# All attention scores of a slice in one block of 96 matmuls over six PSUM banks

## The chip, the cores and the metric

The kernel runs on one core of one Trainium2 chip. The metric is the device time of one execution in microseconds (us), from runs of the whole program; a profile of one more execution shows where the time lies. The engines are called PE (TensorE), DVE (VectorE), ACT (ScalarE), POOL (GpSimd) and SP (SyncE). PE writes its results to PSUM, which has eight banks; DVE and ACT read them from there.

## What is computed

One layer of graph attention over 128 graphs of 128 nodes with 768 features, in 12 heads of 64. The adjacency matrix masks the scores and is added to them as a bias:

```python
# x: (128, 128, 768) f32, adj: (128, 128, 128) f32
h = maximum(layernorm(x), 0)
q, k, v = (split_heads(h @ W + b) for W, b in ((Wq, bq), (Wk, bk), (Wv, bv)))   # W: 768x768
scores = einsum('bhqd,bhkd->bhqk', q, k) / sqrt(64) + beta * adj
scores = where(adj > 0, scores, -9e15)
probs = softmax(scores, axis=-1)
out = x + merge_heads(einsum('bhqk,bhkd->bhqd', probs, v))
```

## The kernel before

The kernel works on 32 groups `G` of four graphs (512 rows). For each group it computes three slices in turn: `qk0` (queries and keys of heads 0 to 5), `v` (values) and `qk1` (queries and keys of heads 6 to 11). A slice is a 3x3 block matrix product by a scheme with 15 block products in place of 27: sums of blocks of activations (names S) and of weights (names T) are multiplied, and each product is added into one of four chains a, b, c, d, which lie in one PSUM bank each. Behind some products of a chain, ACT or DVE takes the chain's running sum into the tiles of the result.

```python
PRODUCTS = (                      # activations, weights, chain, ((block row, block column), sign)
    ("S9", "T9", "c", (((1, 1), -1),)),
    ("A10", "T12", "a", (((1, 0), -1),)),
    ("S10", "T10", "b", (((1, 0), 1),)),
    ("S2", "T2", "c", (((0, 1), -1),)),
    ("S8", "B12", "d", (((1, 1), -1), ((1, 2), 1))),
    # ... fifteen in all; the last of c, a and b are numbers 12, 13 and 14, of d number 8
)

psum = ctx.enter_context(tc.tile_pool(name="psum", bufs=4, space=bass.MemoryType.PSUM))

def product(G, sl, n):
    an, bn, chain, uses = PRODUCTS[n]
    first = all(p[2] != chain for p in PRODUCTS[:n])
    if first:
        banks[chain] = psum.tile([P, 2, H2], F32, tag="mm", name=f"p{chain}_{G}_{sl}")
    p = banks[chain]
    # ... 16 matmuls of 128 x 64 weights by 128 x 256, in halves q of 64 output partitions
    # ... then for each use: ACT (the first of a qk block) or DVE reads the bank
```

The pool has two tags of four banks: `mm` for the chains, `at` for all else (scores, weighted sums, the moments of the layernorm).

Two heads (`oc` is the pair's number) are handled by a pair of functions. `scores` computes query times key, in tiles of 64 x 64 (64 features of a head, 64 keys), for four graphs and two heads: 32 matmuls into two banks, which DVE adds the bias to and ACT takes the exponential of. `attend` multiplies by the values, with the row sum as a 65th column, and divides.

```python
def scores(G, oc):
    u, j = oc // 3, oc % 3
    t = xo[G, oc] = work.tile([P, GRP, P], F32, tag="xo", ...)        # x again, for the residual
    nc.sync.dma_start(t, x[...])
    ps = [psum.tile([P, GRP, N], F32, tag="at", name=f"sc_{G}_{oc}_{i}") for i in range(2)]
    for g in range(GRP):
        t = qk[G, f"qk{u}", g // 2, j]
        at = slice((g % 2) * N, (g % 2 + 1) * N)
        for i in range(2):
            r = slice(i * HD, (i + 1) * HD)
            for k in range(0, N, HD):
                nc.tensor.matmul(ps[i][k:k + HD, g, :], t[r, 1, at][:, k:k + HD], t[r, 0, at],
                                 start=True, stop=True)
    for i in range(2):
        e = es[G, oc, i] = work.tile([P, GRP, N], F32, tag="e", ...)   # four buffers
        nc.vector.scalar_tensor_tensor(e, ps[i], SCORE_CAP * ISCALE, biasT[G], op0=ALU.min, op1=ALU.add)
        nc.scalar.activation(e, e, AF.Exp, scale=1.0 / ISCALE)

def attend(G, oc):
    for r in range(2):
        pa = psum.tile([P, 4, VE], F32, tag="at", name=f"av_{G}_{oc}_{r}")
        # ... 16 matmuls of 128 x 64 weights (e) by 128 x 65 (values), then DVE: weigh()
    # ... POOL adds x, SP stores
```

These are placed between the products of a slice. Heads 0 to 5 (u = 0) of a group are handled in its slice `qk1`, heads 6 to 11 (u = 1) in slice `qk0` of the next group; slice `v` has no attention in it:

```python
def attention(G, u):
    todo = {}
    for i in range(3):
        todo.setdefault(1 + 4 * i, []).append(lambda oc=3 * u + i: scores(G, oc))            # after 1, 5, 9
        todo.setdefault(5 + 4 * i, []).insert(0, lambda oc=3 * u + i: attend(G, oc))         # after 5, 9, 13
    return todo

def slice_of(G, sl, todo, order=range(len(PRODUCTS))):
    for at, n in enumerate(order):
        product(G, sl, n)
        for f in todo.get(at, ()):
            f()
```

Beside this, the slices hold the preparation of the next group: `stats` (DVE, BATCH_NORM_STATS2) late in `qk0`, the moments (a few small matmuls, DVE, POOL) and `norm` (ACT) and the bias from the adjacency in `v`, the transposes of the normed x (DVE) and the sums of its blocks (DVE) in `qk1`. The framework orders the instructions of an engine by these places and by its own estimate of what is ready, so that work without a wait may stand a little earlier. The first group computes its `qk0` plainly (27 block products). The last group has no next slice for its heads 6 to 11 and handles them in half blocks (`scores_half`, 16 matmuls, line L405) within `qk1`.

Of the kernel before, what the change touches and what calls it, by code (L numbers as in the profile page):

```python
# [16 lines left out]
P = 128  # L17
HEADS = 12
GRP = 4
# [77 lines left out]
SLICES = ("qk0", "v", "qk1")  # L97

LAST = (0, 1, 2, 3, 5, 7, 6, 10, 11, 9, 4, 12, 8, 13, 14)

# [6 lines left out]
def direct(ctx, tc, x, adj, wq, bq, wk, bk, wv, bv, beta, out, bad):  # L107
# [27 lines left out]
    stat = ctx.enter_context(tc.tile_pool(name="stat", bufs=4))  # L135
    psum = ctx.enter_context(tc.tile_pool(name="psum", bufs=4, space=bass.MemoryType.PSUM))

# [86 lines left out]
    def moments_1(G, lo, hi):  # L224

        n = hi - lo
        pm[G, lo] = psum.tile([P, 2, n, 2], F32, tag="at", name=f"pm_{G}_{lo}")
        for q in range(0, P, HD):
            nc.tensor.matmul(pm[G, lo][q:q + HD, 0], mean8.rearrange("p a i -> p (a i)")[:, q:q + HD],
                             halves(G, lo, hi, 1), start=True, stop=True)  # L230
# [10 lines left out]
    def moments_2(G, lo, hi, mean, d):  # L241
# [5 lines left out]
        ve = stat.tile([P, n], F32, tag="ve", name=f"ve_{G}_{lo}", bufs=2)  # L247
        nc.vector.tensor_reduce(ve, pm[G, lo][:, 1], AX.X, ALU.add)
        nc.vector.tensor_scalar(ve, ve, -1.0, EPS, op0=ALU.mult, op1=ALU.add)
        r = stat.tile([P, n], F32, tag="rstd", name=f"rstd_{G}_{lo}", bufs=2)  # L250
# [53 lines left out]

    def product(G, sl, n):

        an, bn, chain, uses = PRODUCTS[n]
        first = all(p[2] != chain for p in PRODUCTS[:n])
        if first:
            banks[chain] = psum.tile([P, 2, H2], F32, tag="mm", name=f"p{chain}_{G}_{sl}")  # L310
        p = banks[chain]
        a, b = A[G, an], wt[sl, bn]
# [9 lines left out]
        for (r, j), sign in uses:  # L322
# [14 lines left out]
            elif key not in qk:  # L337
                t = qk[key] = work.tile([P, 2, H2], F32, tag="qk", name=f"{sl}_{G}_{r}_{j}", bufs=10)
                oc = j + 3 * int(sl[2])
# [3 lines left out]
            else:  # L343
                t = qk[key]
                added[G] = nc.vector.tensor_tensor(t, t, p, ALU.add if sign > 0 else ALU.subtract)  # L345

    es, xo = {}, {}

    def scores(G, oc):
        u, j = oc // 3, oc % 3  # L350
        t = xo[G, oc] = work.tile([P, GRP, P], F32, tag="xo", name=f"xo_{G}_{oc}", bufs=3)
        nc.sync.dma_start(t, x[G * GRP:(G + 1) * GRP, :, oc * P:(oc + 1) * P].rearrange("g n d -> n g d"))
        ps = [psum.tile([P, GRP, N], F32, tag="at", name=f"sc_{G}_{oc}_{i}") for i in range(2)]
        for g in range(GRP):
            t = qk[G, f"qk{u}", g // 2, j]
            at = slice((g % 2) * N, (g % 2 + 1) * N)
            for i in range(2):
                r = slice(i * HD, (i + 1) * HD)
                for k in range(0, N, HD):
                    nc.tensor.matmul(ps[i][k:k + HD, g, :], t[r, 1, at][:, k:k + HD], t[r, 0, at],  # L360
                                     start=True, stop=True)
        for i in range(2):
            e = es[G, oc, i] = work.tile([P, GRP, N], F32, tag="e", name=f"e_{G}_{oc}_{i}")
            nc.vector.scalar_tensor_tensor(e, ps[i], SCORE_CAP * ISCALE, biasT[G], op0=ALU.min, op1=ALU.add)  # L364
            nc.scalar.activation(e, e, AF.Exp, scale=1.0 / ISCALE)  # L365

# [11 lines left out]
    def attend(G, oc):  # L378
        o = work.tile([P, 2, 4, HD], F32, tag="o", name=f"o_{G}_{oc}", bufs=2)
        for r in range(2):  # L380
            pa = psum.tile([P, 4, VE], F32, tag="at", name=f"av_{G}_{oc}_{r}")
            for g in range(2):
                for i in range(2):
                    h = 2 * oc + i
                    for q in range(0, P, HD):
                        nc.tensor.matmul(pa[q:q + HD, 2 * g + i, :], es[G, oc, i][:, 2 * r + g, q:q + HD],  # L386
                                         vt[G, "v", r, h // 4][:, 4 * g + h % 4, :], start=True, stop=True)
            weigh(G, oc, r, pa, o[:, r])
        t = xo[G, oc]
        nc.gpsimd.tensor_add(t, t, o.rearrange("p a (b j) d -> p (a b) (j d)", j=2))  # L390
        nc.sync.dma_start(out[G * GRP:(G + 1) * GRP, :, oc * P:(oc + 1) * P].rearrange("g n d -> n g d"), t)

    def scores_half(G, oc, r):
# [4 lines left out]
        nc.sync.dma_start(t, x[g0:g0 + 2, :, oc * P:(oc + 1) * P].rearrange("g n d -> n g d"))  # L398
        ps = [psum.tile([P, 2, N], F32, tag="at", name=f"sc_{G}_{oc}_{r}_{i}") for i in range(2)]
        t = qk[G, f"qk{u}", r, j]  # L400
        for g in range(2):
            for i in range(2):
                h = slice(i * HD, (i + 1) * HD)
                for k in range(0, N, HD):
                    nc.tensor.matmul(ps[i][k:k + HD, g, :], t[h, 1, g * N + k:g * N + k + HD],  # L405
                                     t[h, 0, g * N:(g + 1) * N], start=True, stop=True)
        e = es[G, oc, r] = work.tile([P, 2, 2, N], F32, tag="e", name=f"e_{G}_{oc}_{r}")
        for i in range(2):
            nc.vector.scalar_tensor_tensor(e[:, i], ps[i], SCORE_CAP * ISCALE, biasT[G][:, 2 * r:2 * r + 2, :],
                                           op0=ALU.min, op1=ALU.add)  # L410
            nc.scalar.activation(e[:, i], e[:, i], AF.Exp, scale=1.0 / ISCALE)

    def attend_half(G, oc, r):
        o = work.tile([P, 4, HD], F32, tag="o", name=f"o_{G}_{oc}_{r}", bufs=2)
        pa = psum.tile([P, 4, VE], F32, tag="at", name=f"av_{G}_{oc}_{r}")
# [6 lines left out]
        weigh(G, oc, r, pa, o)  # L422
        t = xo[G, oc, r]
        nc.vector.tensor_add(t, t, o.rearrange("p (b j) d -> p b (j d)", j=2))
# [3 lines left out]
    def attention(G, u):  # L428

        todo = {}  # L430
        for i in range(3):
            todo.setdefault(1 + 4 * i, []).append(lambda oc=3 * u + i: scores(G, oc))
            todo.setdefault(5 + 4 * i, []).insert(0, lambda oc=3 * u + i: attend(G, oc))
        return todo

    def slice_of(G, sl, todo, order=range(len(PRODUCTS))):
        for at, n in enumerate(order):
            product(G, sl, n)
            for f in todo.get(at, ()):
                f()  # L440

    def plain_slice(G, sl, todo):

        n = 0
        for r in range(2):
            for j in range(3):
                p = psum.tile([P, 2, H2], F32, tag="mm", name=f"plain_{G}_{r}_{j}")
                for k in range(3):
# [6 lines left out]
                    if k == 2:  # L455
                        t = qk[G, sl, r, j] = work.tile([P, 2, H2], F32, tag="qk", name=f"{sl}_{G}_{r}_{j}", bufs=10)
                        oc = j + 3 * int(sl[2])
                        for i in range(2):
                            nc.scalar.activation(t[:, i, :], p[:, i, :], AF.Identity, bias=bqk[:, i, oc:oc + 1])
                    for f in todo.get(n, ()):  # L460
                        f()
# [35 lines left out]
    with tc.issue_after(squares[0].ins):  # L497
        warm = psum.tile([P, P], F32, tag="mm", name="warm")
        for n in range(10):
            nc.tensor.matmul(warm, ident, ident, start=True, stop=True)  # L500

# [5 lines left out]
    for G in range(NG):  # L507
        todo = attention(G - 1, 1) if G else {}

        def then(n, f):  # L510
            todo.setdefault(n, []).append(f)

        if G + 1 < NG:
# [15 lines left out]
        else:  # L529
# [3 lines left out]
            slice_of(G, "qk0", todo)  # L533
        todo = {}
        if G + 1 < NG:
            got = []
            at = 1 if G else 6
            for g in range(GRP):
# [12 lines left out]
        slice_of(G, "v", todo)  # L551
        todo = attention(G, 0)

        def transposes(n):
# [31 lines left out]
    nc.vector.tensor_scalar(over[:, 2:3], worst[:, 2:3], (BIAS_CAP * ISCALE) ** 2, None, op0=ALU.is_ge)  # L586
    pf = psum.tile([P, 4], F32, tag="mm", name="pf")
    nc.tensor.matmul(pf[0:1, 0:3], ones, over, start=True, stop=True)
# [133 lines left out]
```

## Time and profile before

| | |
|---|---|
| time, median of 3 runs | 2945.19 us (2944.01 to 2945.37) |
| span of the profiled execution | 2942.0 us |
| PE busy | 2920.4 us, 99% |
| DVE busy | 1993.9 us, 68% |
| ACT busy | 800.1 us, 27% |
| POOL busy | 374.9 us, 13% |
| score matmuls (L360) | 6048, and 96 in half blocks (L405) |
| evacuation of a score bank by DVE (L364) | 682 ns, 378 times |

In the lines of the profile, L320 is a block product, L360 a score matmul, L386 a weighted sum, L364 the DVE instruction that reads a score bank. "128*64" after a matmul is its tile: 128 rows of weights, 64 columns. Tiles are named by the program: pa_qk is chain a in a qk slice, sc a score bank, av a weighted sum, pm the moments. PEld is the loading of weights, which goes on beside the matmuls. Matmuls overlap each other, so the time that a stretch of them takes is read from start to start and not from the length of a line. An arrow points to what an instruction reads or to what it waited for.

### The profile page before, as it was taken

How to read it: one execution, taken by the hardware profiler on the slowest of the kernel's cores; microseconds unless marked ns; L12 is line 12 of the kernel's file. 1: busy time of each engine (PE TensorE's matmuls, PEld its weight loads, DVE VectorE, ACT ScalarE, POOL GpSimd, SP SyncE). 2: the span in 40 equal slices, each digit the busy share in tenths (PEclk: the TensorE clock that was granted, in tenths of full speed). 3: DMA queues.
4: the chain of work that ended last, by engine and by line, in shares of the span. 5: the costliest groups of instructions: out<-in, count | busy, mean ns of one | idle time of the engine just before them, and what ended most of it. 6: DMA issues, size and time to landing. Idle time of an engine off the chain costs nothing.

```text
span 2942.0 us, 81741 instructions
## 1 busy us (share of the span) xinstructions
PE 2920.4 (99%) x35526; PEld 2027.3 (69%) x35526; DVE 1993.9 (68%) x5155; ACT 800.1 (27%) x1703; POOL 374.9 (13%) x307
## 2 busy tenths in 40 slices
PE   8999999999999999999999999999999999999998
PEld 6666666666666666766666666666666676666666
DVE  7866667676676766776666767667676676666665
ACT  1322222323223222222222232222322223222221
POOL 1111111111111111101111111111111110111110
PEclk9999999999999999999999999999999999999999
DMA  5312122121221211221112212122121121211211
GB/s 160 73 52 54 49 63 67 54 55 45 58 70 52 60 47 52 70 61 53 52 47 67 66 52 59 43 60 70 52 59 46 53 69 56 59 47 45 66 38 41
DMA packets 358619, 172.20 MB, mean 59 GB/s; under 512 B 84464, under 2 KB 358128, under 8 KB 358256
## 3 DMA queue, kind: packets, MB, share of 16 engines
q1 hardware_dynamic: 355392, 166.14, 20.5%
q8 instruction: 280, 4.59, 0.6%
q10 hardware_dynamic: 2864, 0.79, 0.1%
q14 instruction: 83, 0.68, 0.1%
HBM read 116.53 MB, written 50.33 MB: 57 GB/s over the span
## 4 chain that ended last, share of the span: by engine, by line
PE 95%; issue 2%; DVE 1%; DMA 1%; ACT 0%; POOL 0%; SPq 0%; POOLq 0%; DVEq 0%
PE pc_qk L320 18%; PE pa_qk L320 15%; PE pb_qk L320 15%; PE pc_v L320 9%; PE pa_v L320 7%; PE pb_v L320 7%; PE pd_qk L320 7%; PE sc L360 6%; PE av L386 6%; PE pd_v L320 4%; PE plain L452 1%; DMA x<-in_x_dram 0%; DVE A L269 0%; ACT x L262 0%; POOL rstd L251 0%
## 5 line engine op out<-in xcount | busy, mean ns | idle before, releaser
L390 POOL TENSOR_TENSOR xo<-xo,o 128x512 f32<-128x512 f32 x189 | 257.0, 1360 | 2266.9 <-DVE seen L376 2208.8
L365 ACT ACTIVATE e<-e 128x512 f32<-128x512 f32 x378 | 232.1, 631 | 713.2 <-DVE e L364 712.4
L262 ACT ACTIVATE x<-x,shift,rstd 128x192 f32<-128x192 f32 x512 | 228.0, 533 | 545.6 <-POOL shift L253 545.6
L320 PE MATMUL pb_qk<-S,qk_T 128*64 128x256 f32 x3024 | 361.7, 381 | 0.0
L341 ACT ACTIVATE qk<-pc_qk,bqk 128x256 f32<-128x256 f32 x378 | 157.6, 467 | 634.9 <-PE pc_qk L320 634.9
L364 DVE SCALAR_TENSOR_TENSOR e<-sc,biasT 128x512 f32<-128x512 f32 x378 | 242.2, 682 | 57.2 <-PE sc L360 57.1
L320 PEld LDWEIGHTS pb_qk<-S,qk_T 128*64 128x64 f32 x3024 | 206.0, 137 | 102.0 <-issue 8.9
L345 DVE TENSOR_TENSOR qk<-qk,pb_qk 128x512 f32<-128x512 f32 x252 | 172.0, 683 | 120.0 <-PE pb_qk L320 119.4
L320 PE MATMUL pc_qk<-S,qk_B 128*64 128x256 f32 x2016 | 243.7, 384 | 3.5 <-ACT qk L341 3.5
L320 PE MATMUL pa_qk<-S,qk_T 128*64 128x256 f32 x2016 | 242.2, 382 | 0.0
L320 PE MATMUL pc_qk<-S,qk_T 128*64 128x256 f32 x2016 | 239.4, 379 | 0.0
L386 PEld LDWEIGHTS av<-v,e 128*64 128x64 f32 x6048 | 208.9, 138 | 27.6 <-issue 0.4
L269 DVE STREAM_TRANSPOSE A<-x 128x256 f32<-128x256 f32 x384 | 218.4, 614 | 7.5 <-ACT x L262 7.4
L360 PE MATMUL sc<-qk 64*64 64x128 f32 x6048 | 208.7, 275 | 0.0
L386 PE MATMUL av<-v,e 128*64 128x65 f32 x6048 | 208.5, 221 | 0.0
L320 PEld LDWEIGHTS pc_qk<-S,qk_T 128*64 128x64 f32 x2016 | 145.0, 137 | 72.8
L320 PEld LDWEIGHTS pc_qk<-S,qk_B 128*64 128x64 f32 x2016 | 139.5, 137 | 79.1 <-issue 11.6
L320 PEld LDWEIGHTS pa_qk<-S,qk_T 128*64 128x64 f32 x2016 | 138.9, 137 | 74.7 <-issue 11.0
L360 PEld LDWEIGHTS sc<-qk 64*64 64x64 f32 x6048 | 163.0, 132 | 32.9 <-issue 24.2
L320 PE MATMUL pb_v<-v_T,S 128*64 128x256 f32 x1536 | 183.4, 380 | 0.0
L219 DVE BATCH_NORM_STATS2 st<-x 128x6 f32<-128x192 f32 x512 | 153.1, 346 | 43.2 <-DMA x<-in_x_dram 38.7
L345 DVE TENSOR_TENSOR qk<-qk,pd_qk 128x512 f32<-128x512 f32 x126 | 86.2, 684 | 129.1 <-PE pd_qk L320 129.1
(117 smaller groups left out, 4221.4 us busy)
## 6 DMA issues: line engine op xcount, KB each, us to landing
x<-in_x_dram SPq DMA_DIRECT2D x504, 96.0 KB, 2.3
xo<-in_x_dram SPq DMA_DIRECT2D x189, 256.0 KB, 2.7
out_dram<-xo SPq DMA_DIRECT2D x189, 256.0 KB, 2.2
adj<-in_adj_dram SPq DMA_DIRECT2D x128, 64.0 KB, 2.4
qk_T<-in_L_gnn_Wq_dram SPq DMA_DIRECT2D x10, 128.0 KB, 3.3
qk_T<-in_L_gnn_Wk_dram SPq DMA_DIRECT2D x10, 128.0 KB, 3.2
v_T<-in_L_gnn_Wv_dram SPq DMA_DIRECT2D x5, 256.0 KB, 5.8
qk_B<-in_L_gnn_Wq_dram SPq DMA_DIRECT2D x8, 128.0 KB, 3.3
```

The lines of the kernel that those rows point to most:

```text
L219: nc.vector.bn_stats(st[G][:, g * NB + b, :], xg[G, g][:, b, :])
L262: nc.scalar.activation(t, t, AF.Relu, bias=shift[G, n], scale=rstd[G, n])
L269: last = nc.vector.transpose(t[:, :, g * N:(g + 1) * N].rearrange("p c (b i) -> p c b i", i=SQ), src)
L320: nc.tensor.matmul(p[q:q + HD, i, :], lhs[:, q:q + HD], rhs, start=(first and i == 0 and c == 0), stop=(c == 1), skip_group_check=True)
L341: nc.scalar.activation(t[:, i, :], p[:, i, :], AF.Identity, bias=bqk[:, i, oc:oc + 1], scale=float(sign))
L345: added[G] = nc.vector.tensor_tensor(t, t, p, ALU.add if sign > 0 else ALU.subtract)
L360: nc.tensor.matmul(ps[i][k:k + HD, g, :], t[r, 1, at][:, k:k + HD], t[r, 0, at], start=True, stop=True)
L364: nc.vector.scalar_tensor_tensor(e, ps[i], SCORE_CAP * ISCALE, biasT[G], op0=ALU.min, op1=ALU.add)
L365: nc.scalar.activation(e, e, AF.Exp, scale=1.0 / ISCALE)
L386: nc.tensor.matmul(pa[q:q + HD, 2 * g + i, :], es[G, oc, i][:, 2 * r + g, q:q + HD], vt[G, "v", r, h // 4][:, 4 * g + h % 4, :], start=Tru ...
L390: nc.gpsimd.tensor_add(t, t, o.rearrange("p a (b j) d -> p (a b) (j d)", j=2))
L452: nc.tensor.matmul(p[:, i, :], b[:, c, i * P:(i + 1) * P], a[:, c, :], start=(k == 0 and i == 0 and c == 0), stop=(c == 1), skip_group_che ...
```

## The change

The three score functions of a slice (three pairs of heads, 32 matmuls each) become one, placed after the second product of the next slice: heads 0 to 5 in slice `v` of the same group (in the first group, in `qk1`), heads 6 to 11 in `qk0` of the next group, as before. It takes six PSUM banks at once and issues 96 score matmuls in a row. It is for having fewer changes between the products' tiles and those of the scores. So that six banks are to be had, the two tags of four banks are given up: the kernel hands out all eight from one queue, and gives each back when its last reader is issued. `attend` goes to places 5, 8 and 11 of the slice. The e buffers become six, the qk buffers eight (from ten), and in slice `v` the moments move from places 1 and 3 to 3 and 6.

```diff
+SC_AT = 1
+AV_AT = (5, 8, 11)
...
-    psum = ctx.enter_context(tc.tile_pool(name="psum", bufs=4, space=bass.MemoryType.PSUM))
+    psum = ctx.enter_context(tc.tile_pool(name="psum", bufs=1, space=bass.MemoryType.PSUM))
+    free = deque(psum.tile([P, W], F32, name=f"bank{i}") for i in range(8))
+    take, give = free.popleft, free.append
... product():
+        mine = [i for i in order if PRODUCTS[i][2] == chain]
+        first = n == mine[0]
         if first:
-            banks[chain] = psum.tile([P, 2, H2], F32, tag="mm", name=f"p{chain}_{G}_{sl}")
+            banks[chain] = take()
...
+        if n == mine[-1]:
+            give(banks.pop(chain))
...
-    def scores(G, oc):
+    def scores(G, u):
+        order = (3 * u, 3 * u + 2, 3 * u + 1)
+        ps = {(oc, i): take() for oc in order for i in range(2)}
+        for oc in order:
+            for g in range(GRP):
+                # ... the same 32 matmuls
             for i in range(2):
-            e = es[G, oc, i] = work.tile([P, GRP, N], F32, tag="e", name=f"e_{G}_{oc}_{i}")
+                e = es[G, oc, i] = work.tile([P, GRP, N], F32, tag="e", name=f"e_{G}_{oc}_{i}", bufs=6)
+                nc.vector.scalar_tensor_tensor(e, ps[oc, i]..., SCORE_CAP * ISCALE, biasT[G], ...)
+                give(ps[oc, i])
+                nc.scalar.activation(e, e, AF.Exp, scale=1.0 / ISCALE)
... attention():
-        for i in range(3):
-            todo.setdefault(1 + 4 * i, []).append(lambda oc=3 * u + i: scores(G, oc))
-            todo.setdefault(5 + 4 * i, []).insert(0, lambda oc=3 * u + i: attend(G, oc))
+        for i, oc in enumerate((3 * u, 3 * u + 2, 3 * u + 1)):
+            todo.setdefault(AV_AT[i] - 3, []).append(lambda oc=oc: load_xo(G, oc))
+            todo.setdefault(AV_AT[i], []).append(lambda oc=oc: attend(G, oc))
... the loop over groups, slice qk0:
+        if G:
+            todo.setdefault(SC_AT, []).insert(0, lambda: scores(G - 1, 1))
... slice v:
-        todo = {}
+        todo = {SC_AT: [lambda: scores(G, 0)]} if G else {}
-            at = 1 if G else 6
+            at = 3 if G else 6
-            then(at + 2, lambda: moments_2(G + 1, 0, GRP * NB, *got[:2]))
+            then(at + (3 if G else 2), lambda: moments_2(G + 1, 0, GRP * NB, *got[:2]))
... slice qk1:
+        if not G:
+            todo.setdefault(SC_AT, []).insert(0, lambda: scores(0, 0))
... slice qk1 of the last group:
-            (0, scores, 0), (3, attend, 0), (3, scores, 1), (6, attend, 1), (6, scores, 2), (9, attend, 2),
+            (0, load_xo, 0), (0, load_xo, 1), (0, load_xo, 2), (0, attend, 0), (2, attend, 2), (4, attend, 1),
```

The rest of the diff makes the other users of PSUM (moments, weighted sums, half blocks, the plain slice) take and give their banks in the same way.

More of the change, by code (lines that the diff above doesn't have):

```diff
@@ L1 @@
 import math
+from collections import deque
 from contextlib import ExitStack
@@ L226, in moments_1 @@
         n = hi - lo
-        pm[G, lo] = psum.tile([P, 2, n, 2], F32, tag="at", name=f"pm_{G}_{lo}")
+        bank = pm[G, lo, "bank"] = take()
+        pm[G, lo] = bank[:, 0:4 * n].rearrange("p (s b h) -> p s b h", s=2, h=2)
         for q in range(0, P, HD):
@@ L248, in moments_2 @@
         nc.vector.tensor_reduce(ve, pm[G, lo][:, 1], AX.X, ALU.add)
+        give(pm[G, lo, "bank"])
         nc.vector.tensor_scalar(ve, ve, -1.0, EPS, op0=ALU.mult, op1=ALU.add)
@@ L303, in direct, with product @@
     banks, added = {}, {}
-    def product(G, sl, n):
+    def product(G, sl, n, order):
         an, bn, chain, uses = PRODUCTS[n]
-        first = all(p[2] != chain for p in PRODUCTS[:n])
+        mine = [i for i in order if PRODUCTS[i][2] == chain]
+        first = n == mine[0]
         if first:
-            banks[chain] = psum.tile([P, 2, H2], F32, tag="mm", name=f"p{chain}_{G}_{sl}")
-        p = banks[chain]
+            banks[chain] = take()
+        p = banks[chain].rearrange("p (i w) -> p i w", i=2)
         a, b = A[G, an], wt[sl, bn]
@@ L337, in product @@
             elif key not in qk:
-                t = qk[key] = work.tile([P, 2, H2], F32, tag="qk", name=f"{sl}_{G}_{r}_{j}", bufs=10)
+                t = qk[key] = work.tile([P, 2, H2], F32, tag="qk", name=f"{sl}_{G}_{r}_{j}", bufs=8)
                 oc = j + 3 * int(sl[2])
@@ L345, in product, with load_xo @@
                 added[G] = nc.vector.tensor_tensor(t, t, p, ALU.add if sign > 0 else ALU.subtract)
+        if n == mine[-1]:
+            give(banks.pop(chain))
     es, xo = {}, {}
-    def scores(G, oc):
-        u, j = oc // 3, oc % 3
+    def load_xo(G, oc):
         t = xo[G, oc] = work.tile([P, GRP, P], F32, tag="xo", name=f"xo_{G}_{oc}", bufs=3)
         nc.sync.dma_start(t, x[G * GRP:(G + 1) * GRP, :, oc * P:(oc + 1) * P].rearrange("g n d -> n g d"))
[L353 to L356, printed above, removed]
-            for i in range(2):
[L358 to L362, printed above, removed]
-            e = es[G, oc, i] = work.tile([P, GRP, N], F32, tag="e", name=f"e_{G}_{oc}_{i}")
-            nc.vector.scalar_tensor_tensor(e, ps[i], SCORE_CAP * ISCALE, biasT[G], op0=ALU.min, op1=ALU.add)
-            nc.scalar.activation(e, e, AF.Exp, scale=1.0 / ISCALE)
+    def scores(G, u):
[3 more added lines that the diff above has]
+            for g in range(GRP):
+                t = qk[G, f"qk{u}", g // 2, oc % 3]
+                at = slice((g % 2) * N, (g % 2 + 1) * N)
+                for i in range(2):
+                    r = slice(i * HD, (i + 1) * HD)
+                    for k in range(0, N, HD):
+                        nc.tensor.matmul(ps[oc, i][k:k + HD, g * N:(g + 1) * N], t[r, 1, at][:, k:k + HD], t[r, 0, at],
+                                         start=True, stop=True)
+            for i in range(2):
+                e = es[G, oc, i] = work.tile([P, GRP, N], F32, tag="e", name=f"e_{G}_{oc}_{i}", bufs=6)
+                nc.vector.scalar_tensor_tensor(e, ps[oc, i].rearrange("p (g n) -> p g n", g=GRP), SCORE_CAP * ISCALE,
+                                               biasT[G], op0=ALU.min, op1=ALU.add)
+                give(ps[oc, i])
+                nc.scalar.activation(e, e, AF.Exp, scale=1.0 / ISCALE)
     def weigh(G, oc, r, pa, o):
@@ L380, in attend @@
         for r in range(2):
-            pa = psum.tile([P, 4, VE], F32, tag="at", name=f"av_{G}_{oc}_{r}")
+            bank = take()
+            pa = bank[:, 0:4 * VE].rearrange("p (b e) -> p b e", e=VE)
             for g in range(2):
@@ L388, in attend @@
             weigh(G, oc, r, pa, o[:, r])
+            give(bank)
         t = xo[G, oc]
@@ L398, in scores_half @@
         nc.sync.dma_start(t, x[g0:g0 + 2, :, oc * P:(oc + 1) * P].rearrange("g n d -> n g d"))
-        ps = [psum.tile([P, 2, N], F32, tag="at", name=f"sc_{G}_{oc}_{r}_{i}") for i in range(2)]
+        ps = [take() for i in range(2)]
         t = qk[G, f"qk{u}", r, j]
@@ L404, in scores_half @@
                 for k in range(0, N, HD):
-                    nc.tensor.matmul(ps[i][k:k + HD, g, :], t[h, 1, g * N + k:g * N + k + HD],
+                    nc.tensor.matmul(ps[i][k:k + HD, g * N:(g + 1) * N], t[h, 1, g * N + k:g * N + k + HD],
                                      t[h, 0, g * N:(g + 1) * N], start=True, stop=True)
-        e = es[G, oc, r] = work.tile([P, 2, 2, N], F32, tag="e", name=f"e_{G}_{oc}_{r}")
+        e = es[G, oc, r] = work.tile([P, 2, 2, N], F32, tag="e", name=f"e_{G}_{oc}_{r}", bufs=6)
         for i in range(2):
-            nc.vector.scalar_tensor_tensor(e[:, i], ps[i], SCORE_CAP * ISCALE, biasT[G][:, 2 * r:2 * r + 2, :],
+            nc.vector.scalar_tensor_tensor(e[:, i], ps[i][:, 0:2 * N].rearrange("p (g n) -> p g n", g=2), SCORE_CAP * ISCALE, biasT[G][:, 2 * r:2 * r + 2, :],
                                            op0=ALU.min, op1=ALU.add)
+            give(ps[i])
             nc.scalar.activation(e[:, i], e[:, i], AF.Exp, scale=1.0 / ISCALE)
@@ L414, in attend_half @@
         o = work.tile([P, 4, HD], F32, tag="o", name=f"o_{G}_{oc}_{r}", bufs=2)
-        pa = psum.tile([P, 4, VE], F32, tag="at", name=f"av_{G}_{oc}_{r}")
+        bank = take()
+        pa = bank[:, 0:4 * VE].rearrange("p (b e) -> p b e", e=VE)
         for g in range(2):
@@ L422, in attend_half @@
         weigh(G, oc, r, pa, o)
+        give(bank)
         t = xo[G, oc, r]
@@ L437, in slice_of @@
         for at, n in enumerate(order):
-            product(G, sl, n)
+            product(G, sl, n, order)
             for f in todo.get(at, ()):
@@ L446, in plain_slice @@
             for j in range(3):
-                p = psum.tile([P, 2, H2], F32, tag="mm", name=f"plain_{G}_{r}_{j}")
+                bank = take()
+                p = bank.rearrange("p (i w) -> p i w", i=2)
                 for k in range(3):
@@ L455, in plain_slice @@
                     if k == 2:
-                        t = qk[G, sl, r, j] = work.tile([P, 2, H2], F32, tag="qk", name=f"{sl}_{G}_{r}_{j}", bufs=10)
+                        t = qk[G, sl, r, j] = work.tile([P, 2, H2], F32, tag="qk", name=f"{sl}_{G}_{r}_{j}", bufs=8)
                         oc = j + 3 * int(sl[2])
@@ L459, in plain_slice @@
                             nc.scalar.activation(t[:, i, :], p[:, i, :], AF.Identity, bias=bqk[:, i, oc:oc + 1])
+                        give(bank)
                     for f in todo.get(n, ()):
@@ L497, in direct @@
     with tc.issue_after(squares[0].ins):
-        warm = psum.tile([P, P], F32, tag="mm", name="warm")
+        warm = take()
         for n in range(10):
-            nc.tensor.matmul(warm, ident, ident, start=True, stop=True)
+            nc.tensor.matmul(warm[:, 0:P], ident, ident, start=True, stop=True)
+        give(warm)
     def behind_adds(f, *args):
@@ L586, in direct @@
     nc.vector.tensor_scalar(over[:, 2:3], worst[:, 2:3], (BIAS_CAP * ISCALE) ** 2, None, op0=ALU.is_ge)
-    pf = psum.tile([P, 4], F32, tag="mm", name="pf")
+    pf = take()
     nc.tensor.matmul(pf[0:1, 0:3], ones, over, start=True, stop=True)
```

## The prediction

> **What bounds the kernel now.** I read the page first, then the waits of TensorE, the timeline of TensorE over one steady slice and over the end, a table of busy time by stage, and the timeline of VectorE. The page:
>
> ```profile
> span 2942.0 us, 81741 instructions
> PE 2920.4 (99%) x35526; PEld 2027.3 (69%) x35526; DVE 1993.9 (68%) x5155; ACT 800.1 (27%) x1703; POOL 374.9 (13%) x307
> ...
> PEclk9999999999999999999999999999999999999999
> ...
> PE 95%; issue 2%; DVE 1%; DMA 1%; ACT 0%; POOL 0%; SPq 0%; POOLq 0%; DVEq 0%
> PE pc_qk L320 18%; PE pa_qk L320 15%; PE pb_qk L320 15%; PE pc_v L320 9%; PE pa_v L320 7%; PE pb_v L320 7%; PE pd_qk L320 7%; PE sc L360 6%; PE av L386 6%; PE pd_v L320 4%; PE plain L452 1%; DMA x<-in_x_dram 0%; DVE A L269 0%; ACT x L262 0%; POOL rstd L251 0%
> ```
>
> TensorE is on 95% of the chain that ended last, at full clock throughout. Its list of waits begins so (columns: total us, times, longest us):
>
> ```profile
> PE pm L229 <- DVE st L219: 7.1, 2, 5.7
> PE pc_qk L320 <- ACT qk L341: 3.5, 1, 3.5
> ```
>
> These are its two longest waits, and both lie in the first 100 us. In the steady part TensorE waits for nobody: time can be won only by giving TensorE less to do or by losing less between its instructions. A busy matmul row does not show such losses, because matmuls overlap; the start times do. The timeline of TensorE at the border of slices qk1 and qk0 (columns: start us, length us, then the instructions merged):
>
> ```profile
> 1018.70 1.10 PE L386 MATMUL av<-v,e 128*64 128x65 f32 x32
> 1019.63 1.90 PE L320 MATMUL pb_qk<-S,qk_T 128*64 128x256 f32 x16
> 1021.36 1.90 PE L320 MATMUL pc_qk<-S,qk_T 128*64 128x256 f32 x16
> 1023.09 1.90 PE L320 MATMUL pa_qk<-A,qk_T 128*64 128x256 f32 x16
> 1024.92 1.10 PE L360 MATMUL sc<-qk 64*64 64x128 f32 x32
> 1025.95 1.95 PE L320 MATMUL pb_qk<-S,qk_T 128*64 128x256 f32 x16
> 1027.73 1.90 PE L320 MATMUL pc_qk<-S,qk_T 128*64 128x256 f32 x16
> ```
>
> From start to start a product of 16 matmuls takes 1.727 us among other products (1021.36 to 1023.09), but 1.827 us when a score block follows (1023.09 to 1024.92: 0.100 us more) and 1.778 us when one came before (1025.95 to 1027.73: 0.051 us more). The weighted sums (av) have the same 128*64 tile as the products and cost no such extra: 1018.70 to 1019.63 is 0.932 us, and the product behind it is again 1.73. Only the scores have the form 64*64.
>
> What a score block costs inside I take from two sizes. One oc has 32 matmuls and takes 1.034 us (1024.92 to 1025.95). The last group has half blocks of 16, here by their starts:
>
> ```profile
> 2917.03 0.67 PE L405 MATMUL sc<-qk 64*64 64x128 f32 x16
> 2917.62 1.95 PE L320 MATMUL pd_qk<-S,qk_B 128*64 128x256 f32 x16
> ```
>
> That is 0.598 us for 16 (the starts unrounded). Sixteen more matmuls cost 1.034 - 0.598 = 0.436 us, or 27.25 ns each, and the part that does not grow is 0.598 - 0.436 = 0.162 us. The single starts in the trace agree: within a block, four matmuls go by every 109 ns, without a break where the block passes to another qk tile.
>
> **What the Trainium skill says.** "TensorEngine Tiling (Array Packing)", Tiling Modes, Key Properties: changing the tiling mode, and not just the tile, drains TensorE. The trace agrees, and gives the price the page lacks: 0.100 + 0.162 + 0.051 = 0.313 us for going into 64*64 and out again. "TensorE: Matmul & The Clock Gate", Part 3, says matmuls on separate tiles run side by side, starting about 4 ns apart; here the four of a group start 6 to 7 ns apart and the next four 109 ns after the first. So the score work itself is already packed, and only the drains are to be won. "PSUM — Partial Sum Buffer", Specifications, gives eight banks of 512 fp32 values a partition: a block of six score banks leaves two for product chains, which is the change's danger.
>
> **What the change removes.** Scores of 189 oc blocks of 32 (6048 / 32) become 63 blocks of 96: 32 for slice qk0 and 31 for qk1 (the last group's qk1 keeps its half blocks). Each takes 0.162 + 96 x 0.02725 = 2.778 us inside, in place of 3 x 1.034 = 3.102, and two of three exits and entries fall away. Per block of 96: 2 x 0.313 = 0.626 us less. 63 x 0.626 = 39.4 us, all on the path, since TensorE is the path. The number of matmuls, weight loads, evacuations and transfers stays.
>
> **What it adds: waits for banks.** Products 0 and 1 of a slice take two banks, the scores six, so product 2 (chain b) must take the bank the first scores leave. Let T be the start of the block. The first two banks are full after 32 matmuls, T + 1.10 us. VectorE empties one in 0.68 us: free at about T + 1.85 if VectorE comes at once. TensorE needs it at T + 2.78. The slack is 0.9 us. Later takers have more: the second score bank is wanted two products later (+3.5 us) and VectorE frees a bank every 0.6 to 0.7 us. At the front the scores need banks of chains c, a and b of the slice before; they are taken last in the block, and chain b's last product was over two products (3.5 us) before the block starts, so VectorE has some 5 us for one 0.68 us instruction.
>
> Does VectorE come at once? By start times over all 31 first score blocks of qk0 slices, the first evacuation starts 1.14 us after the block's start in the median and 1.57 us in nine of ten; later only at the launch. The busy time by stage (a qk0, a v and a qk1 slice; columns: us, then busy time and count of PE, PEld, DVE, ACT, POOL, then clock and DMA):
>
> ```profile
> 1021.36:1053.62 32.26, 32.26 (x435) 22.66 (x432) 22.80 (x71) 9.23 (x19) 4.32 (x5) 1.00 0.24 65
> 1053.62:1079.76 26.14, 26.14 (x252) 17.28 (x250) 11.88 (x22) 7.12 (x16) 4.39 (x3) 1.00 0.07 21
> 1079.76:1112.02 32.26, 32.26 (x436) 22.68 (x434) 28.00 (x71) 8.61 (x18) 3.01 (x2) 1.00 0.29 83
> ```
>
> **What it moves.** The scores of heads 0 to 5 go from slice qk1, where VectorE is fullest (28.0 of 32.26 us), to v, where it is emptiest (11.9 of 26.14). Six evacuations are 6 x 0.68 = 4.1 us. After: qk1 some 23.9 of 32.26 - 3 x (1.034 + 0.151) = 28.7 us; v some 16.0 of 26.14 + 2.93 = 29.07 us; qk0 22.8 of 31.63. No stage comes near to full on VectorE. In v, VectorE now waits for each product:
>
> ```profile
> 1076.52 0.69 DVE L336 TENSOR_TENSOR v<-v,pc_v 128x512 f32<-128x512 f32 x1 [1.04 <-PE pc_v L320]
> 1078.24 0.69 DVE L336 TENSOR_TENSOR v<-v,pa_v 128x512 f32<-128x512 f32 x1 [1.04 <-PE pa_v L320]
> ```
>
> so it will meet the block there at once. ACT does the exponentials early (six of 0.63 us = 3.8) and then the norm, which now starts two to three products later because the moments moved from 1 to 3 and from 3 to 6. By the sum (moments after seven products and the block, about 15.1 us into the slice; 4 us for variance and power; 16 x 0.53 us = 8.5 of norm) it ends near 27.7 us of 29.1. That is close, but it feeds transposes of qk1 whose results TensorE needs only in the next qk0. Three xo loads and stores a slice move too, far from any limit (2.7 us to landing).
>
> **The rivals.**
> 1. A bank wait takes the drains' place. VectorE's queue is in order, and other work may be put ahead of the score evacuations: four BATCH_NORM_STATS2 (1.1 us) or four transposes (2.2 us). If that happened in every qk0 slice, product 2 would wait up to 1.3 us: 31 x 1.3 = 40 us, and the time would be unchanged near 2945. Against it: the median of 1.14 us above. For it: at 1026.0 four such stats did stand ahead of the scores, and the first came 2.14 us after the block's start (free then at T + 2.85: a wait of about 0.1 us).
> 2. The 0.162 us inside a block belongs to each oc (new banks), not to the change of form. Then only 0.151 us is saved 126 times: 19 us, 2926. Against it: the matmuls of a block pass between two banks all the time and cross qk tiles at the same 109 ns.
> 3. The launch gets worse. Between 80 and 125 us VectorE is the bound (it meets the first scores 5.3 us after their start), so the saving is worth nothing there, and six score banks held longer could add 2 to 5 us.
> 4. More than the drains is won. TensorE's waits in all are some 16 us, most of it before 100 us or at the very end; there is nothing else to win, so 2% (59 us) is out of reach.
>
> **The number.** 2945.2 - 39.4 = 2905.8; the launch and a few tenths of a wait in some slices I put at +2: **2908 us**, a ratio of 0.987. The low end, 2900, is the drains in full and a few us of luck at the launch; the high end, 2926, is rival 2, or rival 1 at half strength. Chances: faster by over 2% 0.03, within 2% 0.93, slower by over 2% 0.04 (rival 1 in both v and qk0 with something I don't see).
>
> **What would show it.** Right: 63 score blocks of 96, with 2.78 us to the next start, 1.83 us for the product ahead and 1.78 for the one behind; a period of 90.66 - 2 x 0.626 = 89.41 us for a group of four graphs; no wait of TensorE for VectorE's score evacuation behind a block. Wrong: a gap ahead of product 2 (pb) ended by VectorE; score blocks cut up by products or moments; block time that grows by more than 2.78; a new wait for chain banks at the slice's front.

## The result, and the profile after

The changed kernel takes 2915.24 us (median of 4 runs, 2913.27 to 2918.47) against 2944.6 us before: a ratio of 0.9901, with a 95% interval of 0.9884 to 0.9919. That is 29 us less; the prediction had 2908 and a range of 2900 to 2926. The head of the page of the changed kernel:

```profile
span 2913.8 us, 81848 instructions
PE 2881.5 (99%) x35526; PEld 2017.0 (69%) x35526; DVE 1993.8 (68%) x5155; ACT 796.6 (27%) x1703; POOL 376.0 (13%) x307
```

The counts of instructions and the busy time of DVE are the same. PE has 39 us less, though not one matmul fewer: its row counted the pauses at the change of form as busy. The waits of PE (total us, times, longest us); all users of PSUM are called `bank` now, L331 is a product and L381 the evacuation of a score bank:

```profile
PE bank L331 <- DVE e L381: 11.9, 11, 3.6
PE bank L238 <- DVE st L227: 7.7, 2, 5.8
PE bank L331 <- DVE qk L356: 2.5, 7, 0.9
```

The first line is new: products that wait until DVE has emptied a score bank. The timeline of PE (start us, length us) at a block of 96 (L377) in slice qk0, and then at one in slice v:

```profile
1016.41 1.90 PE L331 MATMUL bank<-A,qk_T 128*64 128x256 f32 x16
1018.24 2.85 PE L377 MATMUL bank<-qk 64*64 64x128 f32 x96
1021.42 3.67 PE L331 MATMUL bank<-S,qk_T 128*64 128x256 f32 x32 [0.33 <-DVE e L381]
...
1048.45 1.90 PE L331 MATMUL bank<-v_T,A 128*64 128x256 f32 x16
1050.27 2.85 PE L377 MATMUL bank<-qk 64*64 64x128 f32 x96
1053.05 3.67 PE L331 MATMUL bank<-v_T,S 128*64 128x256 f32 x32
```

In v the block takes 2.78 us to the next start and the product ahead of it 1.83 us. In qk0 here it is 3.18 us: 0.40 us more, of which the trace puts 0.33 down to the wait for a bank. Over all 63 blocks the medians are 1.827 us for the product ahead, 2.781 us for the block and 1.778 us for the product behind. The busy time by stage, a qk0, a v and a qk1 slice (us; then PE, PEld, DVE, ACT, POOL with counts, clock, DMA):

```profile
1014.69:1046.72 32.03, 31.70 (x434) 22.41 (x432) 22.18 (x64) 9.07 (x19) 5.07 (x5) 1.00 0.30 77
1046.72:1075.78 29.06, 29.06 (x346) 19.97 (x344) 15.52 (x28) 10.75 (x22) 3.13 (x2) 1.00 0.04 11
1075.78:1104.49 28.71, 28.71 (x339) 20.14 (x337) 24.50 (x70) 5.04 (x12) 4.29 (x3) 1.00 0.30 83
```

v and qk1 last what was reckoned (29.07 and 28.7), and VectorE's load has moved from qk1 to v. qk0 is 0.4 us over its 31.63.

To compare the kernels I cut each trace at the starts of products. "Launch" is from the first v product of group 0 to the v slice of group 1. "Steady" is from there to the v slice of group 31 (30 groups, 60 score slices). What is ahead of the launch part differs by up to 3 us from trace to trace (47.7 to 50.8 us), also between kernels that are the same there, and nothing is read from it.

| kernel | us, median | launch | steady | waits in steady qk0, qk1 |
|---|---|---|---|---|
| before | 2944.6 | 96.7 | 2720.2 | 0.0, 1.0 |
| after | 2915.2 | 101.4 | 2690.7 | 5.9, 2.6 |
| banks_only | 2944.0 | 96.1 | 2721.1 | 0.0, 1.9 |
| three_blocks | 2945.8 | 97.6 | 2721.6 | 0.0, 2.1 |
| two_blocks | 2922.4 | 97.4 | 2700.7 | 0.0, 0.0 |
| block_at_0 | 2909.0 | 99.4 | 2683.8 | 0.0, 1.8 |
| stats_behind | 2905.8 | 98.2 | 2682.0 | 0.0, 0.0 |
| behind_and_0 | 2905.6 | 98.5 | 2682.0 | 0.0, 0.0 |
| a12_early | 2909.9 | 102.6 | 2684.1 | 2.1, 0.0 |
| launch_three | 2912.5 | 97.7 | 2689.8 | 6.2, 1.5 |
| behind_launch | 2905.0 | 97.6 | 2682.0 | 0.0, 0.0 |
| form_128 | 3046.4 | 98.6 | 2822.8 | 0.0, 2.3 |

The waits are sums of what the slices take above the median of their kind. In the kernel after, the steady part is 29.5 us shorter, and the launch part 4.7 us longer.

### The profile page after: what moved, and what is told of

Read it like the earlier page. It is cut to its first block, busy times and chain, and to the rows that moved or that the text cites. A ratio compares the mean times of both kernels' runs of the same rounds, so it can differ in the third digit from the quotient of the medians.

```text
span 2913.8 us, 81848 instructions
## 1 busy us (share of the span) xinstructions
PE 2881.5 (99%) x35526; PEld 2017.0 (69%) x35526; DVE 1993.8 (68%) x5155; ACT 796.6 (27%) x1703; POOL 376.0 (13%) x307
## 4 chain that ended last, share of the span: by engine, by line
PE 81%; issue 8%; DVE 5%; DMA 2%; POOL 2%; SPq 1%; ACT 0%; ACTq 0%; POOLq 0%; DVEq 0%
PE bank L331 70%; PE bank L406 5%; PE bank L377 5%; DMA x<-in_x_dram 2%; DVE S L285 1%; PE bank L477 1%; POOL xo L411 1%; POOL rstd L261 1%; DVE qk L356 1%; DVE st L227 1%; DVE A L279 1%; DVE o L392 0%; SPq L152 0%; DVE e L381 0%; ACT x L272 0%
## 5 line engine op out<-in xcount | busy, mean ns | idle before, releaser
L331 PE MATMUL bank<-S,qk_T 128*64 128x256 f32 x7056 | 825.5, 380 | 13.3 <-DVE e L381 11.9
L331 PEld LDWEIGHTS bank<-S,qk_T 128*64 128x64 f32 x7056 | 503.9, 137 | 273.4 <-DVE e L381 16.4
L356 DVE TENSOR_TENSOR qk<-qk,bank 128x512 f32<-128x512 f32 x630 | 430.4, 683 | 347.0 <-PE bank L331 346.7
L352 ACT ACTIVATE qk<-bank,bqk 128x256 f32<-128x256 f32 x756 | 313.4, 471 | 1010.4 <-PE bank L331 870.1
L331 PE MATMUL bank<-S,qk_B 128*64 128x256 f32 x4032 | 478.1, 379 | 0.9 <-DVE qk L356 0.9
L331 PE MATMUL bank<-A,qk_T 128*64 128x256 f32 x4032 | 478.5, 379 | 0.3 <-DVE qk L356 0.3
L331 PE MATMUL bank<-v_T,S 128*64 128x256 f32 x3584 | 422.7, 380 | 0.0
L331 PEld LDWEIGHTS bank<-A,qk_T 128*64 128x64 f32 x4032 | 283.8, 137 | 137.3 <-DVE qk L356 0.4
L331 PEld LDWEIGHTS bank<-S,qk_B 128*64 128x64 f32 x4032 | 278.1, 137 | 129.3 <-DVE qk L356 1.4
L331 PEld LDWEIGHTS bank<-v_T,S 128*64 128x64 f32 x3584 | 252.2, 137 | 126.4 <-issue 5.7
L331 PE MATMUL bank<-v_B,S 128*64 128x256 f32 x2048 | 244.7, 380 | 0.0
L381 DVE SCALAR_TENSOR_TENSOR e<-bank,biasT 128x512 f32<-128x512 f32 x378 | 231.5, 681 | 13.5 <-PE bank L377 13.5
L331 PE MATMUL bank<-v_T,A 128*64 128x256 f32 x2048 | 238.3, 379 | 0.0
L227 DVE BATCH_NORM_STATS2 st<-x 128x6 f32<-128x192 f32 x512 | 160.8, 349 | 76.1 <-DMA x<-in_x_dram 75.6
```

What stands on the lines that cost most here:

```text
L227: nc.vector.bn_stats(st[G][:, g * NB + b, :], xg[G, g][:, b, :])
L331: nc.tensor.matmul(p[q:q + HD, i, :], lhs[:, q:q + HD], rhs, start=(first and i == 0 and c == 0), stop=(c == 1), skip_group_check=True)
L381: nc.vector.scalar_tensor_tensor(e, ps[oc, i].rearrange("p (g n) -> p g n", g=GRP), SCORE_CAP * ISCALE, biasT[G], op0=ALU.min, op1=ALU.add)
```

## The experiments

Two things had to be settled: whether the gain is the change of form (theory) or comes from the new places or the queue of banks (rivals), and what held the rest of it back.

**banks_only.** The eight banks from one queue, everything else as before.

```diff
-        for i, oc in enumerate((3 * u, 3 * u + 2, 3 * u + 1)):      # and AV_AT, SC_AT, moments,
-            ...                                                      # e and qk buffers back as before
+        for i in range(3):
+            todo.setdefault(1 + 4 * i, []).append(lambda oc=3 * u + i: (load_xo(G, oc), scores_one(G, oc)))
+            todo.setdefault(5 + 4 * i, []).insert(0, lambda oc=3 * u + i: attend(G, oc))
```

> The eight banks from one queue, with the old schedule (189 score blocks of 32 at the old places). If the drains of the change of form are the whole gain, this is the kernel before: 2944.6 us less the 2.5 us that the plain slice of the launch won in the trace of the changed kernel, so 2942 (2939 to 2946), with 1.03 us a score block and 1.83 and 1.78 us for the products beside it. If the queue of banks itself brings part of the gain, it is 2935 or less.

Measured: 2943.98 us, ratio 1.0 (0.9991 to 1.0008). The queue by itself is worth nothing. The 2.5 us that I had credited to the plain slice were no gain: that stretch took 50.5 us in the trace of before, 48.1 in that of after and 49.1 here, which is the scatter named above.

**three_blocks and two_blocks.** The block of 96 cut into three of 32 or into 64 and 32, at the front of the same slices. `scores_one` is `scores` for one oc with two banks. two_blocks has the order of stats_behind (below) as well.

```diff
-            todo.setdefault(SC_AT, []).insert(0, lambda: scores(G - 1, 1))
+            [todo.setdefault(n, []).insert(0, lambda oc=oc: scores_one(G - 1, oc)) for n, oc in enumerate((3, 5, 4))]
... the same in slice v, and in qk1 of group 0; two_blocks: a block of two oc behind product 0, of one behind product 1
```

> The changed kernel with its block of 96 cut into three of 32, behind products 0, 1 and 2; places of everything else and the banks as in the change. Drains: 63 x 2 x 0.313 = 39.4 us come back, less the bank waits that fall away because only two banks are taken at a time (6 us in the qk0 slices, up to 6 at the launch): 2942 to 2955. If the gain came from moving the scores to slice v or to the slice's front, it stays at 2910 to 2920.

> As stats_behind (2905.8 us, without bank waits in the steady part), with the block of 96 cut into one of 64 behind product 0 and one of 32 behind product 1. Drains: one more entry and exit a slice, 63 x 0.313 = 19.7 us: 2925.5 (2922 to 2929), half way between one block and three. If not the number of changes of form but the size of the block or its place counts, it is 2905 to 2915 or over 2935.

Measured: 2945.83 us (ratio 1.0007, 0.9998 to 1.0015) and 2922.37 us (0.9928, 0.9915 to 0.9942). In three_blocks all the rest of the change is present and none of the gain. The steady parts give the price: two_blocks less stats_behind is 2700.7 - 2682.0 = 18.7 us over 60 slices, or 0.312 us for one more block; three_blocks less its waits of 2.1 us and less stats_behind is 37.5 us over 120, again 0.312 us. The whole times of two_blocks and stats_behind differ by 16.6 us only, where 19.7 was expected, since the parts outside the steady one differ as well (launch 97.4 against 98.2 us). The timeline of PE in two_blocks (score blocks on L381):

```profile
1045.85 1.90 PE L331 MATMUL bank<-v_T,S 128*64 128x256 f32 x16
1047.67 1.98 PE L381 MATMUL bank<-qk 64*64 64x128 f32 x64
1049.58 1.95 PE L331 MATMUL bank<-v_T,A 128*64 128x256 f32 x16
1051.46 1.10 PE L381 MATMUL bank<-qk 64*64 64x128 f32 x32
1052.49 1.73 PE L331 MATMUL bank<-v_T,S 128*64 128x256 f32 x14
```

The product between two score blocks pays at both ends: 1.88 us from start to start (1049.58 to 1051.46) where 1.73 is the bare price.

**form_128.** The scores in the products' form. They read all 128 rows, so the sum over two heads is computed and the separation of heads is left out.

```diff
-                    r = slice(i * HD, (i + 1) * HD)
-                        nc.tensor.matmul(ps[oc, i]..., t[r, 1, at][:, k:k + HD], t[r, 0, at],
+                        nc.tensor.matmul(ps[oc, i]..., t[:, 1, at][:, k:k + HD], t[:, 0, at],
```

> The changed kernel with the score matmuls in the products' form: they read all 128 rows, so that each score is the sum over two heads (the separation of the heads is left out), same count of matmuls, banks and evacuations. If the 0.313 us belong to the change of form, the product ahead of the block takes 1.727 us, the one behind 1.727, and the block 96 x 54 ns = 5.2 us with nothing on top. If they belong to the switch from products to scores as such (other operands, other banks), 1.83 and 1.78 us remain and the block has 0.16 us on top. The time rises by some 63 x 2.25 = 142 us less the bank waits, to about 3050, either way by the longer matmuls.

Measured: 3046.44 us. The timeline of PE (scores on L376):

```profile
994.69 1.90 PE L331 MATMUL bank<-v_T,A 128*64 128x256 f32 x16
996.42 5.41 PE L376 MATMUL bank<-qk 128*64 128x128 f32 x96
1001.66 1.03 PE L331 MATMUL bank<-v_T,S 128*64 128x256 f32 x8
```

The product ahead takes 1.73 us, the block 5.24 us, and the product behind 1.727 us in the median. The single starts in the block step evenly from the first to the last, at 54.6 ns a matmul, and 96 x 54.6 ns is 5.24 us: nothing comes on top. The tiles, banks and readers are the same, and the 0.313 us are gone: they belong to the form. The block is dearer all the same, as four score matmuls take 109 ns in the form 64*64 and 218 ns in this one.

**stats_behind.** Why does DVE come late in qk0? The timeline of PE at the worst steady block of the changed kernel, then that of DVE:

```profile
1735.20 2.85 PE L377 MATMUL bank<-qk 64*64 64x128 f32 x96
1739.49 0.87 PE L331 MATMUL bank<-S,qk_T 128*64 128x256 f32 x6 [1.44 <-DVE e L381]
```

```profile
1734.55 0.35 DVE L227 BATCH_NORM_STATS2 st<-x 128x6 f32<-128x192 f32 x1
1737.70 1.14 DVE L227 BATCH_NORM_STATS2 st<-x 128x6 f32<-128x192 f32 x4 [2.80 <-DMA x<-in_x_dram]
1738.76 1.87 DVE L381 SCALAR_TENSOR_TENSOR e<-bank,biasT 128x512 f32<-128x512 f32 x3
```

Four stats of the next group stand ahead of the evacuations in DVE's queue. They wait 2.80 us for x from memory, with a full score bank behind them. The edit orders them behind the block's evacuations:

```diff
+    def stats_behind(G, g):
+        with tc.issue_after(evac[0].ins):          # the last evacuation of the slice's score block
+            stats(G, g)
-                    then(11 + g, lambda g=g: stats(G + 1, g))
+                    then(11 + g, lambda g=g: stats_behind(G + 1, g))
```

> The BATCH_NORM_STATS2 of the next group are ordered behind the score evacuations of the qk0 slice on VectorE. If VectorE is late because four of these stats stand ahead of the evacuations and wait for x from memory, every qk0 block's first evacuation starts at 1.14 us and the 6.0 us vanish: 2909 (2906 to 2912). If something else makes VectorE late, the qk0 waits remain: 2913 to 2918; if the stats then come too late for the moments of slice v, it is slower than 2918.

Measured: 2905.82 us, ratio 0.9868 (0.9852 to 0.9883). In all 30 steady qk0 blocks the first evacuation now starts 1.14 us after the block, and the waits in qk0 and in qk1 are both zero. The time is just below the range expected, because the launch part fell too, from 101.4 to 98.2 us, which I had not counted. DVE's timeline at the corresponding block:

```profile
1726.23 0.69 DVE L285 TENSOR_TENSOR S<-A,A 128x512 f32<-128x512 f32 x1
1730.10 3.68 DVE L385 SCALAR_TENSOR_TENSOR e<-bank,biasT 128x512 f32<-128x512 f32 x6 [3.18 <-PE bank L381]
1733.70 0.61 DVE L227 BATCH_NORM_STATS2 st<-x 128x6 f32<-128x192 f32 x2
```

DVE is idle 3.18 us ahead of the scores, which costs nothing, and no longer waits for x.

**a12_early.** The same cause from the other side: bring x sooner and leave the order alone.

```diff
-HT_AT = {"A01": 0, "A00": 1, "A11": 2, "A02": 3, "A10": 4, "A12": 9}
+HT_AT = {"A01": 0, "A00": 1, "A11": 2, "A02": 3, "A10": 4, "A12": 5}
-        ... bufs=1 + (name in ("A01", "A02")))          # xo: bufs=3
+        ... bufs=1 + (name in ("A01", "A02", "A12")))   # xo: bufs=2
```

> The changed kernel with a second buffer for activation block A12, so that its transpose moves from behind product 9 to behind product 5 of slice qk1 and the x buffers of two graphs come free about four products (7.9 us) sooner (an xo buffer less pays for it). If late transfers of x are what holds the stats, and through them the score evacuations, the waits of 6.0 us in qk0 and 2.6 us in qk1 go without any new order on VectorE: 2905 to 2909. If the order on VectorE alone is at fault, they stay: 2913 to 2918.

Measured: 2909.94 us, ratio 0.9883 (0.9868 to 0.9898). Stats still stand directly ahead of the evacuations in 30 blocks, but DVE's waits for x fall from 75.6 to 33.4 us in total. PE's waits fall to 2.1 us in qk0 and 0.0 in qk1. So the late x is the cause, and the order is what passes it on. It was not fully removed here: four qk0 blocks still wait, by up to 1.0 us, and the time is just above the range expected. (The traced execution, 2914.6 us, is the longest of its four; its launch part is 102.6 us.)

What makes x late shows in the chain of work behind the worst block of the changed kernel, the one above (start us, length us; SPq is SyncE; pieces of up to 0.05 us are left out, and one more load at the dots):

```profile
1730.46 1.28 POOL xo L411
1731.76 0.40 SPq L412
1732.21 0.87 SPq L152
...
1733.59 4.09 DMA x<-in_x_dram
1737.70 1.14 DVE st L227 x4
```

POOL adds x for the pair of heads attended at place 11 of qk1, SyncE issues the store of the sum (L412), and 0.05 us behind it come loads of the next group's x (L152), which stand behind that store in SyncE's queue. In the kernel before, the last loads of x went out ahead of such a store (qk0 starts at 1021.36 us here):

```profile
1018.75 1.86 SPq L144 DMA_DIRECT2D x<-in_x_dram  x4
1025.57 0.40 SPq L391 DMA_DIRECT2D out_dram<-xo  x1
```

Over the steady groups of after, the last three of the 16 loads (in one group the last two) stand behind the store, and 2.6 us pass in the median between the load ahead of the store and the store. The last load lands 4.2 us after the start of the qk0 slice (1.4 us in the kernel before). Of the 30 steady qk0 blocks 11 waited: the ten whose last load landed 4.6 us after the start or later, and one other. In a12_early the last transposes end 17.0 us ahead of the slice, in place of 6.3, but the last load still stands behind the store and lands at 3.8 us.

**block_at_0.** More slack for the bank instead: `SC_AT = 0`, so that product 1 takes the eighth bank and product 2 comes 1.73 us later.

> The block of 96 behind product 0 instead of product 1: seven banks are taken then, product 1 gets the eighth, and product 2, which needs the first score bank, comes 1.73 us later. If product 2 waits in the qk0 slices because VectorE is 0.1 to 1.5 us late for that one bank, the 6.0 us there vanish and some of the launch's 6.8: 2905 to 2910. If VectorE is simply overloaded there, the wait moves to a later product and the time stays at 2913 to 2917.

Measured: 2909.04 us, ratio 0.9883 (0.9867 to 0.9898). The qk0 waits are zero, though the first evacuation still starts up to 2.4 us after the block. (The order on DVE moved a little as well: one to three stats stand directly ahead of the evacuations, and the median lateness is 1.32 us in place of 1.88.) The 1.8 us in qk1 stay, as they should if they come from the stats and not from the score banks.

**behind_and_0** has both edits.

> Both remedies: stats behind the evacuations, and the block behind product 0. Steady part as in stats_behind, which has no wait left to remove; only the launch can gain, where product 2 still waits 5.0 us at two blocks: 2901 to 2905 if the bank is what the launch waits for, 2905 to 2907 if VectorE is simply full there and the wait moves.

Measured: 2905.61 us, ratio 0.987 (0.9855 to 0.9885). The steady part is the same to 0.01 us, and the launch part 98.5 us against 98.2. With the stats out of the way, the place of the block no longer matters. In the launch the waits of PE for score banks fall from 5.0 to 3.1 us, but 3.8 us of waits for other work of DVE come in their place: DVE is full there, and the wait moves.

**launch_three and behind_launch.** The first two score blocks alone cut into three, on the changed kernel and on stats_behind.

```diff
+            if G > 1:
                 todo.setdefault(SC_AT, []).insert(0, lambda: scores(G - 1, 1))
+            else:
+                [todo.setdefault(n, []).insert(0, lambda oc=oc: scores_one(G - 1, oc)) for n, oc in enumerate((3, 5, 4))]
... the same in qk1 of group 0
```

> The changed kernel, with the first group's two score blocks alone (in qk1 of group 0 and qk0 of group 1) cut into three of 32, behind products 0, 1 and 2. If the launch loses because product 2 must wait for one of six banks that VectorE, full at that time, empties 5 us late, the time from the first v product to group 1's v slice falls from 101.4 to about 97.7 us (three_blocks had that) although it pays 1.25 us of drains again: 2911.5. If VectorE's own load sets the launch, it stays at 101 and the time at 2915.

> stats_behind with the launch of launch_three: the candidate for the fastest. Steady part as in stats_behind (2682.0 us); the launch falls from 98.2 to 97.7 or less if the bank is the cause: 2904 to 2906, within what can be told from stats_behind's 2905.8 only by the trace. If the launch is VectorE's load alone, the added drains make it 2906 to 2908.

Measured: 2912.46 us (ratio 0.9895, 0.9878 to 0.9911) and 2905.00 us (0.9873, 0.9856 to 0.9889). On the changed kernel the launch part falls from 101.4 to 97.7 us, even with two extra drains paid in each of the two blocks. On stats_behind, which keeps the six banks, it falls by 0.6 us only, from 98.2 us, which the times can't tell. So the six banks alone are not the loss: ordering the stats behind removes 3.2 of the same 3.7 us. The fastest kernels of the study are stats_behind, behind_and_0 and behind_launch, within 1 us of each other.

## Why the prediction was right, and where it was off

- **TensorE is the bound, and its lost time is the drains.** Right. form_128 shows that they belong to the form, three_blocks and two_blocks that they are paid per block: 0.312 us measured against 0.313.
- **63 x 0.626 = 39.4 us on the path.** Right as the sum. stats_behind, where no steady wait is left, saves 2720.2 - 2682.0 = 38.2 us in 60 of the 63 slices (60 x 0.626 = 37.6, and 1.0 us of waits that the kernel before had). Its period of a group is 89.40 us (89.41 predicted). Its time is 2905.8 us, which the prediction gives before its allowance for waits; that the two agree to a tenth is luck, as its launch part is still 1.5 us longer than that of before.
- **Moving the scores to v.** The loads of the stages came out as worked out (v 15.5 us of DVE against 16.0, qk1 24.5 against 23.9), with no wait there: all 30 steady blocks in v were met by DVE at 1.14 us. The norm ended 26.9 us into the slice (27.7 expected). three_blocks shows that the move by itself brings no time.
- **"The launch and a few tenths of a wait in some slices I put at +2."** This term was mis-sized: it measured 2915.2 - 2905.8 = 9.4 us. Between the two traces the span fell by 28.2 us, 11.2 less than 39.4. Waits above those of before are 5.9 us in qk0 and 1.6 us in qk1, and the launch part grew by 4.7 us where the drains should have taken 1.25 off, a loss of 6 us. Against these 13.5 us the stretch ahead of the launch part gave back 2.5 us by its scatter and the end 0.3 us beyond the drains of its one block; some 0.4 us more is spread over the slices.
- **What failed in it** is the step "Does VectorE come at once?", which took DVE's lateness (median 1.14 us) from the trace before. Even there it was not "later only at the launch": two steady blocks were at 1.64 and 2.14 us. In the trace before, four stats also stood directly ahead of 30 score blocks, but x had mostly landed: DVE waited for it 38.7 us in all, after the change 75.6 us. The median lateness rose to 1.88 us and the longest to 3.56 us, against some 2.05 us that the banks allow; 11 of 30 blocks waited. Two parts of the change bring x later. It shortens qk1 by 3.55 us, as three score blocks leave it, and the x buffers come free with the last transposes of qk1, now 6.3 us ahead of the qk0 slice in place of 8.1. And it moves the last `attend` of a slice from place 13 to 11, and the store of that pair now stands ahead of the last loads of x on SyncE. The traces show both; no run undid one of them alone, so their shares stay open.
- **The rivals.** Rival 1 named this wait, and the very instructions, but only a few tenths of it in some slices went into the number; it came at about a sixth of the 40 us written there. A sign of being wrong that was named, a gap ahead of product 2 ended by VectorE, did appear. The range held because its high end allowed for rival 1 at half strength. Rival 2 (cost per oc inside the block) is ruled out by 2.781 us for 96 (it would be 3.10). Rival 3, the launch, came at the upper end of its 2 to 5 us or a little above.

## What to carry to other kernels

Where TensorE is busy throughout, read start-to-start times of equal pieces, sort them by what stands before and behind, and look for pieces that are dearer next to another form; collecting the odd form into one block pays once for each border that is removed. Before counting on a lateness read from the old trace, ask what the change makes shorter and what it moves ahead in a queue: a transfer that was just in time is late when the work that covered it moves away, or when a store that must wait is put ahead of it. Where an engine keeps to its order, as DVE did here with the stats, an instruction that waits for memory should not stand ahead of one that frees a scarce buffer.

## What was not expected of the hardware

A change of form costs the same at every place and size tried: 0.10 us ahead, 0.16 us inside and 0.05 us behind, for blocks of 16, 32, 64 and 96 matmuls. The single starts put the 0.16 us at the two ends of the block: its first four matmuls take 160 ns and its last four 219 ns, where four in the middle take 109 ns. So going in and coming out cost the same, 0.10 to 0.11 us ahead of the change and 0.05 us behind it. A change between the weighted sums (128*64, 65 columns) and the products (128*64, 256 columns) costs nothing measurable. The page's busy row for PE counts the drains as busy; it fell by as much as they were worth, 39 us, when they were taken away, which is a way to see them afterwards.
